# A graph network on one core: blocks of two heads in one double tile, moved by four DMAs, and keys loaded through SP's queue

## The chip, the core and the metric

The kernel runs on one NeuronCore of a Trainium2 chip. The core has TensorE (PE; its weight loads are listed as PEld), VectorE (DVE), ScalarE (ACT), GpSimd (POOL), SyncE (SP), which here only issues DMAs, and 16 DMA engines that all queues share. SP's DMAs are hardware-generated and appear as queue q1, POOL's are software-generated and appear as q0. The metric is the device time of one execution in microseconds; of several runs the median is taken.

## What is computed

Sixteen graphs of 1024 nodes with 256 features go through two layers. Layer 0 is masked attention with 8 heads of 32, layer 1 an edge softmax over the same adjacency, whose entries are 0 or 1 (so only the first of four edge kinds occurs). Cut to what matters:

```python
# layer 0
h = maximum(layernorm(x), 0)
Q, K, V = (h @ W.T + bias, split into 8 heads of 32)
scores = where(adj == 0, -inf, Q @ K.T * 32 ** -0.5)
x = x + (softmax(scores) @ V, heads joined) @ Wo.T + bo
# layer 1
h = maximum(layernorm(x), 0)
e = leaky_relu((h * a_0) @ h.T, 0.2)
x = x + softmax(where(adj == 1, e, -9e15)) @ h
```

## The kernel before

**Steps.** The work is cut into tiles of 128 rows, 8 a batch, 128 in all. After a prelude that projects the whole of batch 0, a loop of 129 steps runs (L838); step s has t = s % 8. In one step four things run beside each other, in an order written out by hand over h = 0 to 7 (L848 to L977): attention of tile s (`now`), the end of attention of tile s - 1 (`was`), layer 1 of the tile nine steps back (`edge`, and the one before it `edge_was`), and layernorm and projection of the tile nine ahead (`piece`, `piece_was`). A tail then does the last edge tiles alone (L984 to L1012). Each engine takes its instructions in the order in which they are written; nothing is reordered.

**One head.** `scores(h)` (L470) is two matmuls of 512 columns into one of two PSUM sides; heads 4 and 6 use side 1, which the edge tile shares, the others side 0. `softmax_max` (L482, DVE) masks and copies the scores to a tile `p`; `softmax_exp` (ACT) follows one h later. Two h later `p` has to be turned, so that PE can multiply it with V. There are two ways. Heads 2, 3, 6 and 7 go through PE and are copied out of PSUM by ACT (`turn_half`, L588). Heads 0, 1, 4 and 5 (`BY_BLOCKS`) are transposed in 32x32 blocks by DVE (`blocks_of`, L393) into a tile of the tag "blocks", and four DMAs on SP's queue (`placed`, L398) then put the blocks of each group of 32 partitions into their place in a tile "pT":

```python
for a in range(NB):
    nc.sync.dma_start(out=pT[:, a * NT * HD : (a + 1) * NT * HD], in_=blocks[a * HD : (a + 1) * HD])
```

Each of these DMAs moves 128 KB. Head 0 is turned at h = 2, head 1 at h = 3, head 4 at h = 6, head 5 at h = 7. `combine(0)` (L525; 64 matmuls, heads 0 to 3) stands at h = 7 of the same step, `combine(1)` (heads 4 to 7) at h = 3 of the next.

**The edge tile.** Its turned tile is made in the same way: `edge_was.turn_blocks` and `place_blocks` at h = 0, one more user of "blocks". A third user is `bend` (L663): at h = 3 ACT writes `less`, which has the tag "blocks" too, and POOL subtracts it in `leak` (L678). "blocks" has three buffers, taken in turn: edge, head 0, `less`, head 1, head 4, head 5. Behind `less` stands `keep(1)` (L643) on ACT, which copies a part of side 1 to `mirror`, and only then may `scores(4)` write side 1.

**POOL.** After `less` POOL runs `sel` (L678), the mask (L454), the split of the projected queries (`halve(1)`, L320), `prepare` (L612), the norms (`norm_of`, L146) and the split of the projected keys (`halve(0)`) of the next step; SP then writes those keys to DRAM (`kd`, L340) before it comes to the edge tile's placements.

**Keys.** Each batch has 8 key tiles of 512 KB, read back from DRAM by `load_key` (L372), on SP's queue for batch 0 and on POOL's for all others. `load_keys` (L841) spreads the eight over the last step of a batch (t = 7: keys 0 to 3, at h = 3 to 6) and the first of the next (t = 0: keys 4 to 7, at h = 0 to 4), by the list

```python
KEY_STEPS = (6, 9, 10, 13, 16, 20, 22, 24)
```

**Other DMAs of a step.** On SP: the query load (512 KB), two query writes (256 KB each), two key writes, the store of x1, the output. On POOL: adjacency (512 KB), two key writes, and three loads of x.

Of the kernel before, what the change touches and what calls it, by code (L numbers as in the profile page):

```python
# [8 lines left out]
F32 = mybir.dt.float32  # L9
# [8 lines left out]
P = 128  # L18
HEADS = 8
HD = 32  # L20
# [6 lines left out]
BY_BLOCKS = (0, 1, 4, 5)  # L27
# [7 lines left out]
FLOOR = 1e28  # L35


def by_chunk(place):
    return place.rearrange("p (c n) -> p c n", n=P)


@with_exitstack
def gnn_kernel(
# [18 lines left out]
    nc = tc.nc  # L62
    B, N, D = x.shape
    NT = N // P
# [124 lines left out]
        nc.vector.bn_aggr(out=mv, in_=st)  # L189


    qds, kds, vs, keysets, weights = {}, {}, {}, {}, {}

    class Piece:

# [4 lines left out]
        def __init__(self, b, first, n=1):  # L200
            self.b, self.first, self.n = b, first, n
            self.cols = slice(first * P, (first + n) * P)
            self.projected, self.halved, self.again, self.queries = [], [], [], []
            self.tags = ("xin", "h0", "hT", "halves", "hTm") if n == 1 else ("pT", "pT", "qt", "p", "blocks")

        def buffer(self, i, shape, dtype=F32):
            tag = self.tags[i]
            if tag == "pT":
                return ptp.tile(shape, dtype, tag=tag, name=tag)
            bufs = {"p": 4, "blocks": 3, "halves": 2 if self.n == 1 else 4, "qt": 2, "xin": 2}.get(tag, 1)  # L210
            return work.tile(shape, dtype, tag=tag, name=tag, bufs=bufs)

        def load(self, queue=nc.gpsimd):
# [158 lines left out]
    def load_key(b, h):  # L372
        kt = keys.tile([P, N], F32R, tag=f"k{h}", name=f"k{h}_{b}")
        c, r = divmod(h, GROUP)
        (nc.sync, nc.gpsimd)[b > 0].dma_start(
            out=kt.bitcast(F32),
            in_=kds[b][c, r * HD : (r + 1) * HD].rearrange("d w u n -> (d w u) n"),
        )
        keysets.setdefault(b, {})[h] = kt
# [10 lines left out]

        return rows.rearrange("(k b) n -> b k n", b=NB)

    def blocks_of(p):  # L393
        blocks = work.tile([P, NB, NT, HD], F32, tag="blocks", bufs=3)
        nc.vector.transpose(blocks.rearrange("p b j q -> p j b q"), p)  # L395
        return blocks.rearrange("p b j q -> p b (j q)")

    def placed(blocks, pT):  # L398
        for a in range(NB):
            nc.sync.dma_start(  # L400
                out=pT[:, a * NT * HD : (a + 1) * NT * HD], in_=blocks[a * HD : (a + 1) * HD]
            )
        return pT.rearrange("p (a j q) -> p j a q", a=NB, j=NT)


    h1s, x1ds, masks = {}, {}, {}
# [22 lines left out]
    class Attend:  # L429
# [65 lines left out]

        def turn(self, h, half):
            if half == 0:
                self.turned[h] = ptp.tile([P, NT, P], F32, tag="pT", name="pT")
            turn_half(self.probs[h][0], self.turned[h], half)

        def turn_blocks(self, h):
            self.blocks = blocks_of(self.probs[h][0])

        def place_blocks(self, h):
            self.turned[h] = placed(self.blocks, ptp.tile([P, N], F32, tag="pT", name="pT"))

        def reciprocals(self):

# [88 lines left out]
    class Edges:  # L597


        def __init__(self, b, t, last=False):  # L600
            self.b, self.t, self.last = b, t, last
            self.rows = slice(t * P, (t + 1) * P)
            self.side = sides[t % 2 if last else 1]
            self.tags = {"sel": ("p", 4), "pT1": ("pT", 7)} if last else {}
            if last and t % 2:
                self.tags |= {"ha": ("hT", 1), "x1b": ("x1", 1)}

# [55 lines left out]
        def bend(self):  # L663

            if not self.last:
                self.less = work.tile([P, N], F32, tag="blocks", name="less", bufs=3)
                nc.scalar.activation(self.less, self.sel, AF.Relu, scale=1 - 1 / SLOPE)  # L667

        def leak(self):
# [119 lines left out]
    with tc.manual_schedule():  # L789
# [195 lines left out]
        gone.turn_normed()  # L985
        gone.turned_normed()
        tiles = [edge_was, edge] + [edges_of(B * NT + LAG - NT + t) for t in range(1, NT)]
        for i in range(1, len(tiles) + 2):
            edge = tiles[i] if i < len(tiles) else None
            if edge:  # L990
                edge.score(0)
                edge.score(1)
            if i <= len(tiles):
                tiles[i - 1].turn_blocks()
                tiles[i - 1].place_blocks()
            if i >= 3:
# [12 lines left out]
            if i >= 2:  # L1009
                tiles[i - 2].gather(0)  # L1010
                tiles[i - 2].gather(1)
# [53 lines left out]
```

## Time and profile before

| | us |
|---|---|
| median of 3 runs (range) | 3232.47 (3231.46 to 3240.4) |
| the profiled execution | 3239.68 |
| its span, clock granted to TensorE | 3237.8, 0.979 |
| PE busy | 2972.1 (92%) |
| ACT, DVE, POOL busy | 2576.2, 2516.9, 2342.7 |
| first score matmul of the loop | at 66.5 |
| placements pT<-blocks on SP's queue | 2560 of 128 KB, median 3.5 from issue to landing |
| key loads on POOL's queue | 120 of 512 KB, median 7.1 |

A busy share is a mean over steps with different limits, so the profile is read here by steps: a step goes from the first score matmul (L474) of one tile to that of the next. Idle time before an instruction is listed with what ended it ("<-DMA pT<-blocks" is the landing of a placement). "SPq" is the issue of a DMA by SP; the time beside it is that of issuing, not of moving. In merged lines of a timeline, x12 is twelve issues in a row.

### The profile page before, as it was taken

The numbers are of one execution on the slowest core, as the hardware profiler recorded it, in microseconds if no ns is written. First come the engines' busy times: TensorE is split into PE (matmuls) and PEld (weight loads), VectorE is DVE, ScalarE is ACT, GpSimd is POOL, SyncE is SP. The second block draws the span as 40 slices with busy tenths as digits, with TensorE's granted clock in tenths as the row PEclk, the third lists the DMA queues.
The fourth block names the chain that finished last, engine by engine and source line by source line (L and its number), as shares of the span: only waits on it lengthen the run. The fifth ranks groups of instructions, "written<-read, shape, count | busy, mean of one in ns | idle before, by whom it ended". The sixth has DMA issues, their size and how long they took to land. (4 is left out here: it accounts for less than half of the span.)

```text
span 3237.8 us, 97791 instructions
## 1 busy us (share of the span) xinstructions
PE 2972.1 (92%) x36210; PEld 2211.2 (68%) x36210; DVE 2516.9 (78%) x4391; ACT 2576.2 (80%) x5157; POOL 2342.7 (72%) x4723
## 2 busy tenths in 40 slices
PE   5878989999899998999999898999989899898987
PEld 3766767667676776767767676776767677676663
DVE  3777868788787887878788787887878788787874
ACT  3887878888787887888888787887878788787871
POOL 2666777777777787777777777787777777776652
PEclk8999999999999999999999999999999999999999
DMA  6787777878878788788878878788888878878663
GB/s 227 222 257 216 232 243 235 256 229 240 248 226 278 223 240 257 232 272 235 260 230 239 258 231 272 220 240 252 234 262 235 262 221 250 258 225 259 186 171 93
DMA packets 747155, 762.91 MB, mean 236 GB/s; under 512 B 71280, under 2 KB 692208, under 8 KB 746672
## 3 DMA queue, kind: packets, MB, share of 16 engines
q1 hardware_dynamic: 678432, 542.34, 56.6%
q0 software_dynamic: 65040, 210.03, 20.6%
q8 instruction: 291, 4.77, 0.6%
q10 hardware_dynamic: 3200, 4.19, 0.4%
q14 instruction: 192, 1.57, 0.1%
HBM read 252.98 MB, written 167.77 MB: 130 GB/s over the span
## 5 line engine op out<-in xcount | busy, mean ns | idle before, releaser
L486 DVE CUSTOM_DVE_ANT_0 p<-s,neg 128x1024 f32<-128x1024 f32 x1024 | 1232.3, 1207 | 273.7 <-PE s L474 192.4
L494 ACT ACTIVATE p<-p,nmx 128x1024 f32<-128x1024 f32 x1024 | 1184.8, 1157 | 156.6 <-DVE nmx L486 154.6
L474 PE MATMUL s<-k,qt 128*128 128x512 f32 x2048 | 766.8, 456 | 145.0 <-DMA qt<-qd 53.5
L395 DVE STREAM_TRANSPOSE blocks<-p 128x1024 f32<-128x1024 f32 x520 | 644.8, 1240 | 152.7 <-DMA pT<-blocks 140.4
L594 ACT COPY pT<-trp 128x512 f32<-128x512 f32 x1024 | 548.4, 590 | 134.1 <-PE trp L593 133.7
L529 PE MATMUL acc<-pT,v 128*32 128x128 f32 x16384 | 552.7, 280 | 42.8 <-DMA pT<-blocks 41.1
L529 PEld LDWEIGHTS acc<-pT,v 128*32 128x32 f32 x16384 | 469.3, 112 | 157.8 <-issue 89.6
L593 PE MATMUL trp<-ident,p 128*128 128x128 f32 x4096 | 549.8, 278 | 2.3 <-ACT pT L594 2.1
L593 PEld LDWEIGHTS trp<-ident,p 128*128 128x128 f32 x4096 | 477.6, 142 | 93.1 <-ACT pT L594 28.8
L454 POOL TENSOR_SCALAR neg<-adj 128x1024 bf16<-128x1024 int32 x128 | 468.8, 3663 | 75.0 <-ACT neg L466 65.1
L700 PE MATMUL acc<-h,pT 128*32 128x256 f32 x8192 | 499.5, 383 | 10.7 <-DVE ot L709 7.8
L474 PEld LDWEIGHTS s<-k,qt 128*128 128x128 f32 x2048 | 326.5, 193 | 253.4 <-issue 87.6
L700 PEld LDWEIGHTS acc<-h,pT 128*32 128x32 f32 x8192 | 244.0, 110 | 216.4 <-issue 59.9
L678 POOL TENSOR_TENSOR sel<-sel,less 128x1024 f32<-128x1024 f32 x120 | 285.7, 2381 | 142.5 <-ACT less L667 142.5
L635 PE MATMUL s<-h1T,ha 128*128 128x512 f32 (+2 forms) x744 | 275.0, 493 | 2.6 <-ACT h1T L572 1.2
L523 ACT COPY recT<-acc 128x256 f32<-128x256 f32 x128 | 47.7, 373 | 205.3 <-PE acc L519 205.3
L494 ACT ACTIVATION_READ_ACCUMULATOR p<-p,nmx 128x1 f32 x1024 | 205.1, 200 | 0.0
L340 POOL DMA_DIRECT2D kd<-halves x240 | 172.1, 764 | 43.1 <-POOL halves L323 34.8
L323 POOL TENSOR_TENSOR halves<-full,halves 128x256 fp32r<-128x256 f32 x240 | 176.4, 735 | 20.6
L635 PEld LDWEIGHTS s<-h1T,ha 128*128 128x128 f32 x744 | 127.7, 192 | 72.0 <-issue 45.6
L273 PEld LDWEIGHTS acc<-hT,wkT 128*128 128x128 f32 x960 | 118.0, 194 | 66.7 <-ACT p L494 31.7
L676 POOL TENSOR_SCALAR less<-top 128x1 f32<-128x1 f32 x120 | 29.8, 248 | 176.7 <-DVE top L658 175.4
(132 smaller groups left out, 4526.9 us busy)
## 6 DMA issues: line engine op xcount, KB each, us to landing
pT<-blocks SPq DMA_DIRECT2D x2560, 128.0 KB, 3.5
qt<-qd SPq DMA_DIRECT2D x128, 512.0 KB, 4.7
adj<-in_adj POOLq DMA_DIRECT2D x127, 512.0 KB, 5.3
qd<-halves SPq DMA_DIRECT2D x240, 256.0 KB, 4.6
k<-kd POOLq DMA_DIRECT2D x120, 512.0 KB, 7.1
kd<-halves POOLq DMA_DIRECT2D x240, 128.0 KB, 3.5
kd<-halves SPq DMA_DIRECT2D x240, 128.0 KB, 3.8
xb<-in_x POOLq DMA_DIRECT2D x128, 128.0 KB, 3.5
```

Source lines behind the costliest of these rows:

```text
L323: nc.gpsimd.tensor_tensor(halves[:, :, 1], self.full, halves[:, :, 0].bitcast(F32), ALU.subtract)
L395: nc.vector.transpose(blocks.rearrange("p b j q -> p j b q"), p)
L454: nc.gpsimd.tensor_scalar(self.neg, self.adj, 0.0, MASKED, ALU.is_equal, ALU.mult)
L474: nc.tensor.matmul(self.ps[:, cols], lhsT=self.qt[:, h, :], rhs=keysets[self.b][h][:, cols], start=True, stop=True,)
L486: nc.vector.tensor_tensor_reduce(out=p, in0=sides[h in (4, 6)], in1=self.neg, scale=-SCALE, scalar=FLOOR, op0=ALU.add, op1=ALU.min, accum_ ...
L494: nc.scalar.activation(p, p, AF.Exp, bias=nmx, scale=-1.0, accum_out=self.sums[:, h : h + 1])
L529: nc.tensor.matmul(sums_place[r * HD : (r + 1) * HD, g * P : (g + 1) * P], lhsT=vs[self.b][:, j, place_of(h) : place_of(h) + HD], rhs=self ...
L593: nc.tensor.transpose(tr[:, j, :], p[:, jj * P : (jj + 1) * P], ident)
L594: copy(pT[:, half * 4 : half * 4 + 4, :], tr)
L635: nc.tensor.matmul(self.side[:, cols], lhsT=self.ha[:, c, :], rhs=h1T[:, c, cols], start=(c == 0), stop=(c == NC - 1),)
L678: nc.gpsimd.tensor_tensor(self.sel, self.sel, self.less, ALU.subtract)
L700: nc.tensor.matmul(sums_place[a * HD : (a + 1) * HD, :], lhsT=self.pT[:, j, a], rhs=h1s[self.b][:, j, :], start=(j == 0), stop=(j == NT - 1),)
```

## The change

- Heads 0 and 1, and 4 and 5, are turned into the two halves of one double tile ("pair", 8 KB a partition, one buffer). Nothing is moved after the first of the two; after the second, four DMAs of 256 KB move both, in rows of 2 KB instead of 1 KB, into a double tile "pairT" (two buffers).
- "pT" has 3 buffers instead of 7, "blocks" 1 instead of 3, for `less` and for the edge tile, which still moves its own blocks by four DMAs of 128 KB.
- All keys are loaded through SP's queue. `KEY_STEPS` is as before.
- The two first pieces of the prelude use halves of the double tiles; in the tail the edge tiles take turns in the halves of one "pair".

```diff
+    def pair(tag):
+        if tag == "pairT":
+            return ptp.tile([P, 2 * N], F32, tag=tag, name=tag, bufs=2)
+        return work.tile([P, 2 * N], F32, tag=tag, name=tag, bufs=1)
...
-            self.tags = ("xin", "h0", "hT", "halves", "hTm") if n == 1 else ("pT", "pT", "qt", "p", "blocks")
+            self.tags = ("xin", "h0", "hT", "halves", "hTm") if n == 1 else ("pairT", "pairT", "qt", "p", "pair")
...
-            if tag == "pT":
-                return ptp.tile(shape, dtype, tag=tag, name=tag)
-            bufs = {"p": 4, "blocks": 3, "halves": 2 if self.n == 1 else 4, "qt": 2, "xin": 2}.get(tag, 1)
+            if tag in ("pair", "pairT"):
+                if i not in shared:
+                    shared[i] = pair(tag)
+                half = by_chunk(shared[i], N)[:, self.first // self.n].bitcast(dtype)
+                return half.rearrange("p (a b) -> p a b", a=shape[1])
...
-        (nc.sync, nc.gpsimd)[b > 0].dma_start(
+        nc.sync.dma_start(
             out=kt.bitcast(F32),
...
-    def blocks_of(p):
-        blocks = work.tile([P, NB, NT, HD], F32, tag="blocks", bufs=3)
-        nc.vector.transpose(blocks.rearrange("p b j q -> p j b q"), p)
-        return blocks.rearrange("p b j q -> p b (j q)")
-
-    def placed(blocks, pT):
+    def blocks_of(p, blocks, i, n):
+        blocks = blocks.rearrange("p (b h j q) -> p h j b q", h=n, b=NB, j=NT)
+        nc.vector.transpose(blocks[:, i], p)
+
+    def placed(blocks, pT, n):
+        width = n * NT * HD
         for a in range(NB):
             nc.sync.dma_start(
-                out=pT[:, a * NT * HD : (a + 1) * NT * HD], in_=blocks[a * HD : (a + 1) * HD]
-            )
-        return pT.rearrange("p (a j q) -> p j a q", a=NB, j=NT)
+                out=pT[:, a * width : (a + 1) * width],
+                in_=blocks[a * HD : (a + 1) * HD].rearrange("s (b n) -> s b n", b=NB),
+            )
+        return pT.rearrange("p (a h j q) -> p h j a q", a=NB, h=n, j=NT)
...
-                self.turned[h] = ptp.tile([P, NT, P], F32, tag="pT", name="pT")
+                self.turned[h] = ptp.tile([P, NT, P], F32, tag="pT", name="pT", bufs=3)
...
         def turn_blocks(self, h):
-            self.blocks = blocks_of(self.probs[h][0])
+            i = BY_BLOCKS.index(h) % 2
+            if i == 0:
+                self.blocks = pair("pair")
+            blocks_of(self.probs[h][0], self.blocks, i, 2)
 
         def place_blocks(self, h):
-            self.turned[h] = placed(self.blocks, ptp.tile([P, N], F32, tag="pT", name="pT"))
+            if BY_BLOCKS.index(h) % 2:
+                pT = placed(self.blocks, pair("pairT"), 2)
+                self.turned[h - 1], self.turned[h] = pT[:, 0], pT[:, 1]
...
-            self.tags = {"sel": ("p", 4), "pT1": ("pT", 7)} if last else {}
+            self.tags = {"sel": ("p", 4), "pT1": ("pT", 3)} if last else {}
...
-                self.less = work.tile([P, N], F32, tag="blocks", name="less", bufs=3)
+                self.less = work.tile([P, N], F32, tag="blocks", name="less", bufs=1)
...
-        def turn_blocks(self):
-            self.blocks = blocks_of(self.sel)
+        def turn_blocks(self, place=None):
+            if place is None:
+                place = work.tile([P, N], F32, tag="blocks", name="blocks", bufs=1)
+            self.blocks = place
+            blocks_of(self.sel, place, 0, 1)
 
         def place_blocks(self):
-            self.pT = placed(self.blocks, self.buffer("pT1", [P, N]))
+            self.pT = placed(self.blocks, self.buffer("pT1", [P, N]), 1)[:, 0]
...
+        sets = by_chunk(pair("pair"), N)
...
-                tiles[i - 1].turn_blocks()
+                tiles[i - 1].turn_blocks(sets[:, i % 2])
```

More of the change, by code (lines that the diff above doesn't have):

```diff
@@ L35, with by_chunk @@
 FLOOR = 1e28
-def by_chunk(place):
-    return place.rearrange("p (c n) -> p c n", n=P)
+def by_chunk(place, n=P):
+    return place.rearrange("p (c n) -> p c n", n=n)
 @with_exitstack
@@ L189, in stats_of @@
         nc.vector.bn_aggr(out=mv, in_=st)
-    qds, kds, vs, keysets, weights = {}, {}, {}, {}, {}
+    qds, kds, vs, keysets, weights, shared = {}, {}, {}, {}, {}, {}
+    def pair(tag):
+        if tag == "pairT":
+            return ptp.tile([P, 2 * N], F32, tag=tag, name=tag, bufs=2)
+        return work.tile([P, 2 * N], F32, tag=tag, name=tag, bufs=1)
     class Piece:
@@ L203, in __init__ @@
             self.projected, self.halved, self.again, self.queries = [], [], [], []
-            self.tags = ("xin", "h0", "hT", "halves", "hTm") if n == 1 else ("pT", "pT", "qt", "p", "blocks")
+            self.tags = ("xin", "h0", "hT", "halves", "hTm") if n == 1 else ("pairT", "pairT", "qt", "p", "pair")
         def buffer(self, i, shape, dtype=F32):
             tag = self.tags[i]
-            if tag == "pT":
-                return ptp.tile(shape, dtype, tag=tag, name=tag)
-            bufs = {"p": 4, "blocks": 3, "halves": 2 if self.n == 1 else 4, "qt": 2, "xin": 2}.get(tag, 1)
+            if tag in ("pair", "pairT"):
[3 more added lines that the diff above has]
+                return half.rearrange("p (a b) -> p a b", a=shape[1])
+            bufs = {"p": 4, "halves": 2 if self.n == 1 else 4, "qt": 2, "xin": 2}.get(tag, 1)
             return work.tile(shape, dtype, tag=tag, name=tag, bufs=bufs)
```

## The prediction

> **What bounds the kernel now.** I read the table by stretches first, cut at the first score matmul (L474) of each of the eight steps of one batch, steps 72 to 79 of the loop. Columns: stretch, its length, then busy time of PE, PEld, DVE, ACT and POOL, the granted clock, the DMA share and GB/s.
>
> ```profile
> 1794.13:1824.87 30.74, 23.40 (x285) 18.28 (x286) 19.06 (x35) 19.65 (x40) 21.23 (x44) 0.89 0.85 291
> 1824.87:1849.19 24.32, 23.77 (x286) 16.91 (x283) 19.57 (x35) 20.64 (x44) 17.14 (x32) 1.00 0.77 230
> 1849.19:1872.77 23.58, 23.18 (x288) 17.11 (x284) 19.47 (x35) 20.47 (x43) 18.15 (x37) 1.00 0.80 240
> ...
> 1896.04:1919.03 22.99, 22.59 (x289) 17.05 (x285) 19.56 (x35) 20.03 (x41) 18.09 (x37) 1.00 0.79 232
> ...
> 1941.93:1964.41 22.48, 22.35 (x287) 16.77 (x284) 19.50 (x35) 20.02 (x41) 18.06 (x36) 1.00 0.77 221
> 1964.41:1987.77 23.36, 21.88 (x288) 16.96 (x284) 19.45 (x35) 20.11 (x41) 18.42 (x34) 1.00 0.90 267
> ```
>
> Two regimes are to be seen. In steps t = 1 to 6 PE is busy for all but about 0.4 us: TensorE sets the step. The first step of a batch (t = 0) has the same PE work and lasts 7 us longer. Who is late there, the waits say (engine and line, what it waited for, us in all, times, longest):
>
> ```profile
> DVE blocks L395 <- DMA pT<-blocks: 140.4, 80, 5.0
> PE s L474 <- DMA qt<-qd: 53.5, 22, 15.2
> PE acc L529 <- DMA pT<-blocks: 41.1, 25, 5.1
> PE s L474 <- DMA k<-kd: 39.9, 23, 3.9
> PE s L474 <- ACT mirror L649: 31.2, 83, 0.7
> ACT less L667 <- DMA pT<-blocks: 26.1, 9, 5.3
> ```
>
> PE waits for keys, placed blocks and queries; all come by DMA, and the DMA view of the stretch 1794 to 1825 us shows a share of 0.9 or more at 350 to 400 GB/s for its first 16 us, with 5.1 us instead of 3.6 from issue to landing of a placed block. I average the steps by their place, batches 1 to 14, from the same starts: t = 0 to 7 last 30.30, 24.46, 23.59, 23.27, 23.00, 23.14, 22.79 and 24.80 us, a batch 195.35.
>
> The third view is the timeline of step 76 (t = 4; start, us, engine, line), for a chain that does not bind today but will matter:
>
> ```profile
> 1898.87 0.74 POOL L323 TENSOR_TENSOR halves<-full,halves 128x256 fp32r<-128x256 f32 x1
> 1900.90 1.25 SPq L340 DMA_DIRECT2D kd<-halves  x2
> 1902.26 10.01 SPq L400 DMA_DIRECT2D pT<-blocks  x12
> ...
> 1905.65 1.05 ACT L667 ACTIVATE less<-sel 128x1024 f32<-128x1024 f32 x1
> 1906.60 0.57 ACT L649 COPY mirror<-s 128x512 f32<-128x512 f32 x1
> 1906.78 2.38 POOL L678 TENSOR_TENSOR sel<-sel,less 128x1024 f32<-128x1024 f32 x1 [1.23 <-ACT less L667]
> 1907.22 0.73 PE L474 MATMUL s<-k,qt 128*128 128x512 f32 x2 [0.40 <-ACT mirror L649]
> ...
> 1921.87 0.74 POOL L323 TENSOR_TENSOR halves<-full,halves 128x256 fp32r<-128x256 f32 x1
> ```
>
> The first four of the twelve placements from 1902.26 are the edge tile's. They land about 1907.8, after `less` has begun: `less` takes another of the three "blocks" buffers. PE's scores(4) waits for the mirror copy that stands behind `less` on ACT, and POOL's `sel` waits for `less`.
>
> **The change, part by part.**
>
> *Fewer placements.* Sixteen head placements a step become eight of 256 KB. Four cost SP 2.5 us in the timeline (0.64 each), so SP is free 5 us earlier a step; edge tiles keep four small ones. In step 76 SP came to the key writes (1900.90) 1.3 us after their data (1899.61); the time of heads 4's and 5's placements did that. This alone moves nothing in steps 1 to 6, since PE hides it. For the packets: the queues' rows give 56.6% of 16 engines' span for 542 MB on q1, 54 us of engine time per MB, and 51 on q0. At q0's price the 2 MB of heads would save 6 us of engine time a step, 0.4 us over 16 engines; I take 0 to 0.4, all under PE. [...]
>
> *DVE.* The 520 transposes of 1240 ns remain. Heads 1 and 5 wait for no buffer now; heads 0 and 4 wait until the single double tile has been read. Head 5 ends 0.6 us into the step, four issues follow to 3.2, and a 256 KB write lands 4.6 us after its issue (the row of qd), so 7.2; head 0 begins at 6.5 today. So 0.7 us, in place of 0.98 before head 1 in step 76. DVE is idle over 3 us a step: cost nothing, and 0.7 us a step if that cover were gone. PE's combine(1) at 8.6 still finds its data.
>
> *Keys on SP's queue.* 120 issues of 575 ns (69 us) and 25 us of waits leave POOL. What counts is when they go out: POOL issues keys 1 and 2 late, behind the mask (3.66 us) and the norms. On SP they stand behind the query load, some 4 to 5 us earlier, key 3 before the step ends. Keys 4 to 6 follow at the start of t = 0, with the key writes, the edge placements and the double placement queued behind them; key 0 waits for the last key writes, and then the pair's placement, 3 us away, stands behind it. In steps 7 and 0 a normal 5.3 MB each (the DMA view of step 76) and 4 MB of keys have to move: 14.7 MB, 38 us at 390 GB/s, beside 45.3 us of PE work (21.88 + 23.40). So the stall of t = 0 need not be, if the load is spread. [...]
>
> *"blocks" has one buffer, not three.* The order of the changed program's instructions shows `less` waiting for the four edge placements of its own step. This adds a wait with much behind it on ACT: the mirror copies (PE's scores(4)), the flag, exp(3); and POOL's `sel`. It closes a **loop**: from the end of `less` (1906.70) POOL works without a pause, sel, mask, halves, ha, norms, until the next halves end (1922.62): 15.92 us, the same in steps 2 to 6. Then SP's two key writes 1.36 and three placement spacings 1.92 (3.3 in all), landing 3.6, `less` 1.05. The sum is 23.9 us, whatever PE has to do. The landing is the uncertain term: 2.5 is the shortest block placement in the trace, 5.1 the median in the full queue of t = 0; I take 3.6, the median of step 76, since the same bytes go out in the same order.
>
> *pT from 7 to 3 plus two double ones; first pieces and tail in halves of double tiles.* A pT is freed by the combine before its next use (combine(0) ends the step, head 2 comes at h = 4). Cost 0; if one were short, a turn would wait for a combine, 2.2 us.
>
> *Sum.* t = 1: 24.2 (PE 23.8 and 0.4). t = 2 to 7: 23.9 each, 143.4. t = 0: the loop, one key issue ahead (0.6) and 5.1 instead of 3.6 to land: 26.0. A batch: 193.6 instead of 195.35, 1.75 us less, 14 times: 25. The last batch's edges have no key writes ahead; its first step gives 2 more at most, which I leave out. The profiled execution took 3239.7 us (span 3237.8, 1.9 around it), 7 over the median of the runs shown, 3232.5; the same saving against that gives **3207**.
>
> **Rivals.**
> - *The new wait wins (slower).* From a landing of 3.9 us the loop of 24.2 in all seven steps and 26 for the first eat the gain. At 4.3, a loop of 24.6: 172.2 + 26 = 198.2, 2.85 more a batch, 40 us: 3272. For it: 1 MB of pair goes out just ahead, and kd lands after up to 4 us there. Against: SP is 1.3 us earlier.
> - *The wait hardly binds.* With 3.1, a loop of 23.4: 24.2 + 23.55 + 5 x 23.4 + 25.5 = 190.25, 5.1 less a batch, 71 us: 3161. For it: queue and SP are emptier.
> - *The keys still collide.* One queue in order makes blocks wait behind keys; half of what t = 0 gives is lost, 28.2 instead of 26.0: 195.8, 0.45 more a batch: 3239. This is also the case that the change does not do what it says.
>
> **How the numbers follow.** Likeliest, 3195 to 3222: 0.36. Rival one 0.34; rival two 0.17; rival three 0.13. Faster is the first with rival two, less a little at its edge: 0.5; within 0.3% (10 us, about what a measurement of this kernel can tell) 0.14; slower 0.36. The range reaches over most of both sides: 3145 to 3290; the likeliest alone is 3195 to 3222.
>
> **What would show it.** Right: t = 0 shrinks to about 26 us; steps 2 to 7 all become equally long, near 23.9, with PE gaps behind the mirror copy and `less` waiting for the DMA of blocks in some hundred steps; DVE's wait for blocks falls under heads 1; POOL's L375 is gone. Wrong: steps 2 to 6 stay at 22.5 to 23.6 (no loop), or t = 0 stays near 30 (keys still late), or DVE waits long before head 0.

## The result, and the profile after

The changed kernel takes **3766.26 us** (median of four runs, 3761.83 to 3780.7) where the kernel before, run beside it, takes 3236.43 us: ratio **1.164, 95% interval 1.160 to 1.168**. The prediction was 3207 with a range to 3290, so it is wrong in sign and size. The profiled execution took 3768.68 us, its span is 3766.6 us, and the clock granted to TensorE fell from 0.979 to 0.926. The loop's place in the program is the same; only line numbers moved: scores are L483 now (L474 before), placements L408 (L400), turnings L403 (L395), `less` L681 (L667), the mirror copy L663 (L649), the key writes L348 (L340), the combine L543 (L529).

The stretches of the changed kernel, steps 72 to 79, cut as before (length, busy time of PE, PEld, DVE, ACT, POOL, granted clock, DMA share, GB/s):

```profile
2100.89:2130.76 29.87, 23.42 (x290) 17.04 (x286) 19.37 (x35) 19.77 (x40) 18.31 (x37) 0.94 0.93 305
2130.76:2158.75 27.99, 25.05 (x286) 18.20 (x283) 19.57 (x35) 21.07 (x44) 18.41 (x38) 0.94 0.71 193
2158.75:2188.56 29.81, 25.30 (x287) 19.00 (x283) 19.57 (x35) 20.90 (x43) 18.95 (x39) 0.89 0.70 183
...
2216.23:2243.00 26.77, 23.74 (x290) 18.07 (x286) 19.38 (x35) 20.14 (x41) 17.07 (x31) 0.94 0.72 185
...
2298.30:2327.97 29.67, 25.54 (x289) 20.02 (x285) 19.48 (x35) 20.15 (x41) 20.32 (x46) 0.83 0.88 248
```

The two regimes are gone. From t = 1 on no engine fills a step any more, the DMA share is lower than before (0.70 to 0.72 in the three rows shown of t = 1, 2 and 4, 0.77 to 0.80 before), and yet steps t = 1 to 6 of this batch are 3.7 to 6.2 us longer. By their place, batches 1 to 14, the steps t = 0 to 7 last 30.00, 28.55, 29.51, 27.69, 27.53, 29.06, 28.24 and 27.65 us, a batch 228.24 instead of 195.35. Batch 0, whose steps have no edge tile in the loop, grew too, from 20.5 to 25.9 us a step. The 32.89 us of 14 batches (460), 8 steps of batch 0 (43), batch 15 (17) and the tail (8) make up the whole 529 us between the two spans.

The waits of the changed kernel (engine, line, what it waited for, us in all, times, longest):

```profile
ACT less L681 <- DMA pT<-blocks: 398.0, 98, 7.9
DVE pair L403 <- DMA pairT<-pair: 352.5, 115, 6.3
...
PE s L483 <- ACT mirror L663: 284.3, 99, 4.9
...
PE acc L543 <- DMA pairT<-pair: 160.0, 95, 4.8
```

There are two kinds: `less` on ACT waits for the edge tile's placements (the wait that the prediction saw coming), and DVE (head 0) and PE (the combine) wait for the double placement (which it priced at nothing). The timeline of step 76 shows both; the step begins at 2216.23:

```profile
2215.61 1.24 DVE L403 STREAM_TRANSPOSE pair<-p 128x1024 f32<-128x1024 f32 x1
2216.91 3.98 SPq L408 DMA_DIRECT2D pairT<-pair  x4
2217.50 0.73 POOL L331 TENSOR_TENSOR halves<-full,halves 128x256 fp32r<-128x256 f32 x1
2220.99 3.18 SPq L348 DMA_DIRECT2D kd<-halves  x2
2224.28 2.97 SPq L408 DMA_DIRECT2D pT<-blocks  x4
2226.80 1.25 DVE L403 STREAM_TRANSPOSE pair<-p 128x1024 f32<-128x1024 f32 x1 [3.97 <-DMA pairT<-pair]
2226.81 0.30 PE L543 MATMUL acc<-pairT,v 128*32 128x128 f32 x2 [1.95 <-DMA pairT<-pair]
2229.61 1.06 ACT L681 ACTIVATE less<-sel 128x1024 f32<-128x1024 f32 x1 [3.67 <-DMA pT<-blocks]
2231.19 0.73 PE L483 MATMUL s<-k,qt 128*128 128x512 f32 x2 [1.08 <-ACT mirror L663]
```

SP issues the four placements of heads 4 and 5 from 2216.91 on; single ones show that the third and the fourth issue take 1.27 and 1.37 us instead of 0.6, and the last lands at 2226.68. That is 9.8 us after the first issue. At that moment DVE's head 0 and PE's combine(1) go on. SP reaches the key writes at 2220.99, 2.8 us after their data (2218.23), and needs 3.2 us for these two; so the edge tile's placements start at 2224.28 and `less` at 2229.61, 13.4 us into the step instead of 9.6 in the same step before.

### The profile page after: what moved, and what is told of

Read it like the earlier page. It is cut to its first block, busy times and chain, and to the rows that moved or that the text cites. A ratio compares the mean times of both kernels' runs of the same rounds, so it can differ in the third digit from the quotient of the medians.

```text
span 3766.6 us, 95108 instructions
## 1 busy us (share of the span) xinstructions
PE 3110.6 (83%) x36210; PEld 2331.7 (62%) x36210; DVE 2519.5 (67%) x4391; ACT 2597.2 (69%) x5157; POOL 2285.5 (61%) x4603
## 5 line engine op out<-in xcount | busy, mean ns | idle before, releaser
L483 PE MATMUL s<-k,qt 128*128 128x512 f32 x2048 | 815.9, 482 | 367.3 <-ACT mirror L663 284.3
L403 DVE STREAM_TRANSPOSE pair<-p 128x1024 f32<-128x1024 f32 x520 | 644.6, 1240 | 444.2 <-DMA pairT<-pair 352.5
L543 PE MATMUL acc<-pairT,v 128*32 128x128 f32 x8192 | 535.8, 287 | 205.2 <-DMA pairT<-pair 160.0
L543 PEld LDWEIGHTS acc<-pairT,v 128*32 128x32 f32 x8192 | 465.1, 115 | 306.8 <-issue 140.2
L483 PEld LDWEIGHTS s<-k,qt 128*128 128x128 f32 x2048 | 347.8, 205 | 489.2 <-ACT mirror L663 329.4
L607 PE MATMUL trp<-ident,p 128*128 128x128 f32 x4096 | 608.7, 298 | 26.3 <-ACT pT L608 26.2
L607 PEld LDWEIGHTS trp<-ident,p 128*128 128x128 f32 x4096 | 543.8, 155 | 122.1 <-ACT pT L608 39.1
L543 PE MATMUL acc<-pT,v 128*32 128x128 f32 x8192 | 535.8, 287 | 0.0
L681 ACT ACTIVATE less<-sel 128x1024 f32<-128x1024 f32 x120 | 126.8, 1057 | 474.6 <-DMA pT<-blocks 398.0
L543 PEld LDWEIGHTS acc<-pT,v 128*32 128x32 f32 x8192 | 454.0, 115 | 0.0
L649 PE MATMUL s<-h1T,ha 128*128 128x512 f32 (+2 forms) x744 | 272.8, 490 | 2.7 <-ACT h1T L586 2.4
L564 DVE TENSOR_TENSOR x<-acc,xb 128x256 f32<-128x256 f32 x128 | 54.4, 425 | 285.9 <-ACT full L326 215.6
L348 POOL DMA_DIRECT2D kd<-halves x240 | 172.2, 762 | 41.4 <-POOL halves L331 34.5
```

The lines of the kernel that those rows point to most:

```text
L348: queue.dma_start(out=kds[self.b][oc, :, :, twice, self.cols], in_=halves.rearrange("p (w n) -> p w n", w=2),)
L403: nc.vector.transpose(blocks[:, i], p)
L483: nc.tensor.matmul(self.ps[:, cols], lhsT=self.qt[:, h, :], rhs=keysets[self.b][h][:, cols], start=True, stop=True,)
L543: nc.tensor.matmul(sums_place[r * HD : (r + 1) * HD, g * P : (g + 1) * P], lhsT=vs[self.b][:, j, place_of(h) : place_of(h) + HD], rhs=self ...
L607: nc.tensor.transpose(tr[:, j, :], p[:, jj * P : (jj + 1) * P], ident)
L649: nc.tensor.matmul(self.side[:, cols], lhsT=self.ha[:, c, :], rhs=h1T[:, c, cols], start=(c == 0), stop=(c == NC - 1),)
```

## The experiments

**By themselves: how fast is such a move (runs 1 and 5)?** In run 1 nothing but SP's queue runs; in run 5 POOL's queue loads 512 KB at a time beside some of the bursts.

> The placements by themselves: nothing is computed (the output is zeros), SP's queue alone moves 4 MB in each of six forms, once as one long burst and three times as a burst of 1 MB. Forms: rows of 1 KB as in the kernel before (32 partitions read, 128 KB each); the same out of a double tile; rows of 2 KB as in the changed kernel (32 partitions read, 256 KB each); these with the groups in the order 0, 2, 1, 3; 256 KB with 1 KB rows; 256 KB with 2 KB rows read from all 128 partitions. Theory one (a transfer that reads 32 partitions is slow in itself once 256 KB go out every 0.64 us): the third form lands its fourth placement about 10 us after the first issue, as in step 76 of the changed kernel (9.8), with packets near 147 ns, while the one that reads 128 partitions lands it by about 5 to 6 us with packets near 84 ns; the first form lands 1 MB at SP's spacing, 8 x 0.64 + 3, about 8 us. Rival (the transfer is slowed by the other traffic of the step, not by its own form): the third form alone has packets of 84 ns and lands by 5 to 6 us, like the sixth. [...]

The fourth placement of 256 KB out of 32 neighbouring partitions lands 7.1 to 7.3 us after the first issue, its packets last 84 ns (median), 148 on average and over 300 the slowest tenth, and SP's third and fourth issue take 1.2 and 1.6 us. Read from 128 partitions, the same bytes in the same rows land 4.3 us after the first issue, nearly every packet takes 84 to 93 ns, every issue 0.5 to 0.6 us. In a long burst one of 256 KB comes down every 1.14 us from neighbours (15 in 17.14 us, **229 GB/s**) and every 0.68 us (SP issues one every 0.65) from 128 partitions. In the order 0, 2, 1, 3 it is every 1.05 us, 9% more; its three short bursts took 6.4, 6.7 and 7.6 us. 128 KB placements, at SP's 0.65 us, ask for 201 GB/s, stay under this and land after 2.6 us each. Eight of them are down after 7.1 us, no later than four of 256 KB. So theory one holds in this: the move out of 32 neighbouring partitions is slow by itself, though not the 10 us of the kernel. Rows of 1 KB in a DMA of 256 KB are as slow (1 MB after 7.2 to 7.4 us), so the row's length is not what made the difference here.

> Placements by themselves again, nothing computed (the output is zeros). 256 KB out of 32 partitions in rows of 2 KB to 128 partitions, once from 32 neighbouring partitions (as in the changed kernel), once from every fourth partition (32 partitions spread over all 128); and 128 KB in rows of 1 KB. Then each form behind one load of 512 KB and two writes of 256 KB on the same queue and one load of 512 KB on POOL's. Theory one (neighbouring partitions share the way out of SBUF): spread over all, the transfer keeps SP's spacing, issues take 0.6 us, the fourth lands 5 us after the first issue (7.2 from neighbours), packets 84 ns. Rival (32 source partitions, or four rows out of each, are slow wherever they lie): the same 7.2 in both. Behind the other traffic the fourth placement of 256 KB lands 2 to 3 us later than alone, that is about as late as in the kernel (9.8).

```python
in_=src[a * HD : (a + 1) * HD]    # neighbours
in_=src[a::NB]                    # every fourth partition
```

These are the DMA views of two long bursts of 4 MB with SP's queue alone, neighbours first (run 1), then every fourth partition (run 5), each in 40 slices (of the 21.1 and 13.6 us); the last line of each gives the median from issue to landing:

```profile
GB/s 0 0 74 105 136 245 120 93 303 307 210 260 245 210 206 210 225 284 256 163 148 256 326 214 210 322 264 214 136 237 342 233 148 202 249 280 206 182 136 0
dst<-src SPq DMA_DIRECT2D x16, 256.0 KB, 4.7
```

```profile
GB/s 0 0 0 145 386 374 386 368 386 380 392 380 386 386 386 386 386 386 373 380 386 362 392 380 380 392 374 361 398 374 392 380 386 380 386 343 18 0 0 0
dst<-src SPq DMA_DIRECT2D x16, 256.0 KB, 2.7
```

Each DMA of both reads 32 partitions, 8 KB of each, and writes the same rows. Spread over all 128 they run at 380 GB/s from start to end, and the fourth of a short burst lands 4.4 us after the first issue (5.1 in one burst, where the second issue came late), against 7.1 to 7.3 out of neighbours. So it was where the 32 partitions lie that counted here, not how many they are. Out of neighbours the rate starts at some 100 GB/s and then swings between 90 and 340.

The other traffic was not tested as it was meant. All nine of POOL's loads went out early, beside the neighbours' bursts at the start of the run, and SP's load had landed before the placements began. Beside one of POOL's loads the fourth placement out of neighbours lands 7.6 to 8.3 us after the first issue; right behind two writes of 256 KB alone, 7.4 to 7.6. What makes it 9.8 us in step 76 (9.2 is the median of heads 4 and 5 over batches 1 to 14, 8.2 in batch 0) is open by 1 to 2 us.

**The keys alone (run 2).** The kernel before with only `load_key` changed.

```diff
-        (nc.sync, nc.gpsimd)[b > 0].dma_start(out=kt ...
+        nc.sync.dma_start(out=kt ...
```

> The kernel before with one part of the change: the keys on SP's queue. Theory one (keys are not what slowed the changed kernel): within 40 us of the kernel before; if the prediction's step on keys holds, t = 0 falls from 30.3 to about 26 us and the time by 14 x 4, to about 3180. Rival (keys on SP's queue hold up the placements behind them): t = 0 and t = 7 grow by 5 us or more each, 3236 + 14 x 10, about 3380.

Ratio 1.010 (1.006 to 1.014). Step t = 7 falls from 24.80 to 22.74, t = 0 grows from 30.30 to 34.32, where PE waits 7.3 us for keys (2.6 before). SP issues key 3 only 5.1 us into the step and key 7 at 22.1, each behind the placements that are written ahead of it. So the keys cost 28 us, within the 40 of theory one and a sixteenth of the loss; t = 0 did not fall to 26 us.

**The wait of `less` alone (run 3).** The kernel before; `less` and the edge tile's blocks share one buffer, heads keep two.

```diff
-  self.less = work.tile([P, N], F32, tag="blocks", name="less", bufs=3)
+  self.less = work.tile([P, N], F32, tag="blocks1", name="less", bufs=1)
-  self.blocks = blocks_of(self.sel)             # tag "blocks", bufs=3
+  self.blocks = blocks_of(self.sel, "blocks1", 1)
```

> The kernel before with one part of the change: less and the edge tile's blocks share one buffer (heads keep two, the sum is three as before), so less has to wait for the edge placements of its own step. Theory one (this wait is late only because the double placements hold up SP and the queue): the loop of the prediction, 23.9 us a step, 3 us a batch more than now, 3236 + 14 x 3, about 3280. Rival (this wait is the main cause): steps of 27 us and more, 3236 + 113 x 3.5, above 3600.

Ratio **1.114** (1.109 to 1.119): the rival is right, this wait is dear without any double placement. A batch takes 219.20 us; batch 0, which has no edge tile, is unchanged (20.9 a step). `less` waits 345.7 us in 99 steps and starts at 11.1 to 12.1 us in t = 1 to 6. SP's timeline of step 44, which starts at 1207.75, shows why:

```profile
1207.44 1.36 SPq L400 DMA_DIRECT2D pT<-blocks  x2
1208.84 0.60 SPq L555 DMA_DIRECT2D x1d<-x  x1
1209.55 2.49 SPq L400 DMA_DIRECT2D pT<-blocks  x4
1212.14 1.24 SPq L340 DMA_DIRECT2D kd<-halves  x2
1213.49 8.75 SPq L400 DMA_DIRECT2D pT<-blocks  x11
```

The four from 1209.55 are head 5's. Only after them, 4.4 us into the step, SP comes to the key writes and then to the edge tile. In steps t = 2 to 6 this start lies 4.6 to 5.1 us into the step in the kernel before, in this one and in the changed one (medians), and here 1.3 to 3.2 us after the key data: it follows heads 4 and 5, not POOL. The prediction had it at once behind POOL.

**Head 5 behind the edge tile (run 9).** As run 3, with head 5's placements issued after the key writes and the edge placements of the next step.

```diff
-                    turning.place_blocks(th)
+                    if th != 5:
+                        turning.place_blocks(th)
...
                         edge_was.place_blocks()
+                    if was:
+                        was.place_blocks(5)
```

> The third run again (the kernel before, less and the edge tile's blocks in one buffer), with one thing moved: SP issues the four placements of head 5 after the key writes and the edge tile's placements of the next step, not before them. Theory (the loop that set that run's steps goes from scores(4) over the step's end, head 5's turning and its four issues on SP to the key writes, which start 4.8 us into the step in every kernel): the key writes start right after their data, the loop is POOL's, 15.92 + 0.2 + 1.36 + 1.94 + 3.5 + 0.1 + 1.06 = 24.1 us, about 3270 to 3340. Rival (this wait is dear wherever head 5's placements stand): 3560 to 3650, as in the third run.

Ratio 1.126 (1.124 to 1.129). The expected time is missed by far, yet the wait did move as the theory says. The waits of this run:

```profile
PE acc L529 <- DMA pT<-blocks: 425.8, 122, 8.4
...
ACT less L667 <- DMA pT<-blocks: 88.9, 20, 8.2
```

The key writes start 0.03 to 1.2 us behind their data and `less` stands where it stood before the change (9.0 to 10.9 us into the step), but head 5 now lands 13.7 us into step 44, and combine(1), which precedes scores(4) on PE, waits for it. One of the two has to be late on SP; this run could not tell the price of the buffer.

**Without head 5's placements (runs 13 and 14).** So they were left out, in two kernels, one with the shared buffer and one without.

```diff
-                    turning.place_blocks(th)
+                    if th == 5:
+                        turning.turned[5] = turning.turned[4]
+                    else:
+                        turning.place_blocks(th)
```

> The third run (the kernel before, less and the edge tile's blocks in one buffer) without the placements of head 5: the combine takes head 4's turned tile for head 5 as well, so the output is another, DVE, ACT and PE have the same instructions, SP has four issues and the queues 512 KB less a step. Theory (less is late there because SP comes to the key writes and the edge placements only after head 5's four issues): the key writes start within 0.3 us of their data and the steps are POOL's loop, 15.92 + 0.3 + 1.36 + 1.94 + 3.4 + 0.1 + 1.06 = 24.1 us, 60 to 110 us above the same kernel with three shared buffers, about 3280 to 3330. Rival (the single buffer is dear whatever stands ahead on SP): 250 us or more above it.

> The kernel before without the placements of head 5 (the combine takes head 4's turned tile), to measure the thirteenth run against: buffers as before. PE sets most steps: 3195 to 3240 by every theory.

Ratios 1.049 (1.047 to 1.052) with one buffer and 0.984 (0.982 to 0.987) with three, the latter 9 us below its expected range; 209 us between the medians (3395.3 and 3185.9), between what the two theories gave. With one buffer SP starts the key writes 0.03 us behind their data (median), and t = 2 to 6 last 24.0 to 25.1 us. The sum of the loop with what this run shows (landing 3.9) is 15.92 + 0.03 + 1.32 + 1.92 + 3.9 + 0.1 + 1.06 = 24.25. So POOL's loop is real and about as long as the prediction said; it takes 1.7 us a step from t = 2 to 6 (24.7 against 23.05) and 5.5 us more in t = 0 and 7 together. The other 150 us of run 3 go with head 5's four placements. This run takes away their issues on SP and their 512 KB at once; that SP then starts right behind the data speaks for the issues, but the two were not tested apart.

**The same bytes in eight DMAs (run 4).** The changed kernel; each half of the double tile goes by itself.

```diff
-        for a in range(NB):
-            nc.sync.dma_start(
-                out=pT[:, a * width : (a + 1) * width],
-                in_=blocks[a * HD : (a + 1) * HD].rearrange("s (b n) -> s b n", b=NB),
-            )
+        for i in range(n):
+            for a in range(NB):
+                nc.sync.dma_start(
+                    out=pT.rearrange("p (a h x) -> p h a x", a=NB, h=n)[:, i, a],
+                    in_=blocks[a * HD : (a + 1) * HD].rearrange("s (b h x) -> s h b x", b=NB, h=n)[:, i],
+                )
```

> The changed kernel with the double tile moved by eight DMAs of 128 KB in rows of 1 KB instead of four of 256 KB in rows of 2 KB; tiles, buffers, the moment of the first issue and the bytes stay. Theory one (the 2 KB form is slow in itself: 147 ns a packet, where two of 1 KB take 2 x 54): the placements land some 1.5 us earlier and SP's key writes and the edge placements are no longer slowed, less comes about 1 us earlier, about 3600 to 3680. Rival (what counts is that both heads' bytes start only after the second head, whatever their form): 5.1 us of issues instead of 3.9 ahead of the key writes, 3766 to 3880.

Ratio **1.065** (1.060 to 1.070), 318 us under the changed kernel and better than expected. The expectation was wrong in one thing that decides how this is read: the first issue does move. The first four DMAs read the first head's half only, so SP waits for that head's turning and issues them 1.47 us before the step instead of 0.68 us into it. The run undoes two things, the size and the late start. The placements of heads 4 and 5 are then down 7.2 us into the step, at 9.85 in the changed kernel (medians of batches 1 to 14). Batch 0 is back at 20.5 us a step. Stretches of two steps of batch 0, the changed kernel first, then this one:

```profile
142.88:168.02 25.14, 18.90 (x214) 15.51 (x210) 16.01 (x29) 16.98 (x36) 13.85 (x30) 0.91 0.68 183
168.02:194.47 26.45, 19.77 (x213) 16.10 (x210) 17.15 (x30) 18.22 (x38) 13.85 (x30) 0.82 0.66 176
```

```profile
126.84:147.42 20.58, 18.13 (x214) 14.79 (x210) 16.59 (x29) 17.64 (x37) 13.58 (x31) 0.92 0.76 229
147.42:168.01 20.59, 18.15 (x214) 14.80 (x211) 16.61 (x30) 17.63 (x37) 14.01 (x31) 0.92 0.76 221
```

PE is busy 0.8 and 1.6 us longer in the changed kernel, at a clock of 0.91 and 0.82 instead of 0.92; the rest of the 4.6 and 5.9 us are gaps, and the DMA rate is lower, not higher.

**`less` with a buffer of its own**, in both forms (runs 6 and 7); 4 KB of it are paid for with two "pT" instead of three.

```diff
-  ... tag="pT", name="pT", bufs=3)
+  ... tag="pT", name="pT", bufs=2)
-  ... tag="blocks", name="less", bufs=1)
+  ... tag="blocks", name="less", bufs=2)
...
-  place = work.tile([P, N], F32, tag="blocks", name="blocks", bufs=1)
+  place = work.tile([P, N], F32, tag="blocks", name="blocks", bufs=2)
```

> The changed kernel with eight DMAs of 128 KB for the double tile (as in the fourth run) and two buffers for blocks, so that less waits for no placement of its own step; paid for with two pT instead of three. What is left of the change: both heads start after the second, one pair, keys on SP. Theory (the form of the transfers and the wait of less are all, the keys cost 30 us, the bunching nothing): the time of keys alone, 3260 to 3300. Rival (bunching, or the single pair, costs as well): above 3350.

> The changed kernel, four DMAs of 256 KB as in the change, but two buffers for blocks (less waits for no placement of its own step) and two pT instead of three. Theory (the 256 KB form hurts by itself too, as batch 0 shows, where no less waits: 25.9 us a step instead of 20.5): 3550 to 3650. Rival (the form hurts only by making the placements that less waits for late): 3260 to 3330.

With eight DMAs: ratio **0.995** (0.993 to 0.998), a little faster than the kernel before, and below what was expected. With four of 256 KB: 1.117 (1.115 to 1.120), as expected. Again the eight start early, so the first of the two says nothing on what bunching would cost. Together with run 4 and the changed kernel this is a table of two by two, as ratios to the kernel before:

| | `less` waits for the edge tile | own buffer |
|---|---|---|
| four of 256 KB, after the second head | 1.164 | 1.117 |
| eight of 128 KB, four of them early | 1.065 | 0.995 |

The form (size and late start together) costs 12.2% alone, the wait 7.0% alone, both together 17.0%, less than their sum. Without them nothing of the loss is left. How the form works alone, the waits of run 7 say:

```profile
DVE pair L403 <- DMA pairT<-pair: 370.9, 148, 6.4
ACT less L681 <- DVE top L672: 323.9, 107, 6.5
...
PE acc L543 <- DMA pairT<-pair: 172.8, 95, 4.9
```

`less` waits for no placement there, but for DVE's maximum of the edge tile (`top`), which stands behind head 0, and head 0 waits for the pair: so `less` still starts 12.3 us into the step (median of t = 1 to 6; 13.7 in the changed kernel, 9.8 before).

**Another order (run 8).** The changed kernel with `for a in (0, 2, 1, 3)`.

> The changed kernel, only the order of the four placements is 0, 2, 1, 3 instead of 0, 1, 2, 3 (double tile and edge tile). By themselves four of 256 KB landed 6.6 us instead of 7.2 after the first issue in this order. Theory (two neighbouring transfers out of the same half of the partitions share the same way): 0.6 us less twice a step on the chain, 3766 - 113 x 0.6 to 1.2, that is 3630 to 3700. Rival (the way out is not what makes them late in the kernel): 3750 to 3780.

Ratio 1.142 (1.139 to 1.144), 64 us under the changed kernel and, at 3702 us, just above the expected 3630 to 3700. The placements of heads 4 and 5 are down at 9.24 instead of 9.85 us. So 0.61 us of landing is worth 64 us, 0.57 us in each of 113 steps; the 2.62 us between the changed kernel and the run with eight DMAs are worth 318, 2.8 us a step. Both would fit a step that follows this landing about one to one. But `less` starts earlier in both as well, 13.1 and 11.4 us into the step instead of 13.7, so these runs do not tell the two waits apart.

**Keys again, and a version that beats both (runs 10 to 12 and 15 to 18).** In the run with eight DMAs and `less` of its own, SP is free at the end of a step: head 4's placements stand one h later in its order than in the kernel before, and keys 1 to 3 go out 6.5, 5.8 and 1.3 us before step t = 0 begins. In the run with the keys alone, keys 1 and 2 go out 4.9 and 4.1 us before it and key 3 5.1 us into it. In all the runs below that have eight DMAs, four of the eight start early, as in run 4, so none of them tests the bunching.

> The kernel before with keys 0 to 3 (those of t = 7) on SP's queue and keys 4 to 7 (those of t = 0) on POOL's. Theory (keys on SP help t = 7, where they don't stand behind POOL's mask, by 2 us a batch, and hurt t = 0, where they stand behind placements, by 4): 3236 - 14 x 2, about 3205 to 3225. Rival (the 4 us of t = 0 come from the same bytes being moved, not from where the keys of t = 0 stand): 3250 to 3280.

> The sixth run (eight DMAs of 128 KB, two buffers for blocks, keys on SP) with keys 4 to 7 on POOL's queue. If keys behind placements are what holds t = 0, below the sixth run by 1 to 3 us a batch, 3185 to 3215; if the bunching had already cured that (t = 0 is 28.9 us there, 34.3 with the keys alone), the same as the sixth run, 3220 to 3240, or a little more.

> The sixth run with all keys of later batches on POOL's queue, as in the kernel before. What is left of the change is then only that both heads of a pair are moved after the second. Theory (bunching itself costs nothing and gains nothing): 3230 to 3250, the kernel before. If the sixth run's gain comes from keys on SP that meet fewer placements on their way: the gain is lost, 3236 or more; if it comes from the bunching: below 3226.

> The sixth run once more, with more rounds and beside the next: 3220 to 3235, 0.3 to 0.6% under the kernel before.

> The sixth run with the keys of t = 0 issued earlier on SP's queue (KEY_STEPS 16, 18, 20, 22 instead of 16, 20, 22, 24). PE waits 2.5 us a batch for keys in t = 0 there. If what makes them late is where they stand on SP, 1 to 2 us less a batch: 14 to 28 us under the sixth run, about 3200 to 3212. If the queue is simply full in t = 0: the same time, 3220 to 3235.

> The sixteenth run with the keys of t = 0 still earlier on SP's queue (KEY_STEPS 15, 16, 18, 20). If they are late for their place on SP alone, another 0.5 to 1 us a batch, 3180 to 3192; if the transfers of t = 7 and t = 0 then meet and delay placements, 3200 to 3230.

> The kernel before with the key times of the sixteenth run (KEY_STEPS 16, 18, 20, 22), keys on POOL's queue as before. If early keys gain by themselves, 14 to 28 us here too, 3210 to 3225; if they gain only where SP's queue has room for them (both heads moved after the second, keys on SP), 3230 to 3250.

| | ratio (interval) | t = 7 | t = 0 |
|---|---|---|---|
| before, keys 0 to 3 on SP | 1.000 (0.998 to 1.002) | 22.51 | 31.95 |
| eight DMAs, own `less`, keys 0 to 3 on SP | 1.001 (1.000 to 1.003) | 22.78 | 30.25 |
| the same, keys on POOL | 1.002 (1.000 to 1.003) | 23.34 | 30.41 |
| the same, keys on SP (run 6 again) | 0.997 (0.995 to 0.999) | 22.96 | 29.49 |
| the same, keys on SP, steps 16, 18, 20, 22 | **0.988** (0.985 to 0.990) | 23.03 | 27.29 |
| the same, steps 15, 16, 18, 20 | 0.986 (0.983 to 0.990) | 22.92 | 26.96 |
| before, keys on POOL, steps 16, 18, 20, 22 | 0.999 (0.997 to 1.002) | 25.31 | 30.28 |

Keys on SP pay only in the version in which SP is free for them, and earlier keys only there: 40 us under the kernel before (3196.4 and 3236.6); in the kernel before they were tried on POOL's queue alone. Of the keys that run 16 moves, two go out nearly as in run 15 (11.6 and 12.9 us into t = 0 on average, 11.8 and 13.0 there) and the last 7 us earlier (13.4 instead of 20.6); PE's wait for keys in t = 0 falls from 3.0 to 1.2 us. Half of the keys on SP gains nothing in either place, so both expectations of run 10 missed, and in run 11 the one of a gain. The next step earlier is worth nothing more that could be measured (run 17, 3199 us, just under the upper of its two expected ranges). Three steps of the version with steps 16, 18, 20, 22, t = 0, 1 and 3 of one batch:

```profile
1772.17:1799.12 26.95, 22.18 (x289) 16.71 (x285) 19.38 (x35) 19.77 (x40) 18.57 (x39) 1.00 1.00 333
1799.12:1823.45 24.33, 23.78 (x286) 16.92 (x282) 19.57 (x35) 20.65 (x44) 17.89 (x35) 1.00 0.75 217
1847.80:1871.07 23.27, 22.87 (x289) 17.21 (x285) 19.59 (x35) 20.28 (x42) 18.12 (x37) 1.00 0.81 239
```

PE fills t = 1 and 3 again, and t = 0 is near the 26.0 of the prediction.

## Why the prediction was wrong, step by step

- *What bounds the kernel now*: right, and what was left after both faults were removed is bound by it again.
- *Fewer placements*: wrong. SP did not become free 5 us earlier. Four issues fewer save 2.5 us a pair in number, but the third and fourth of 256 KB take 1.3 us each, and SP came to the key writes as late as before (4.8 us into the step). The packets' gain of 0 to 0.4 us is a loss: one of 2 KB takes 147 ns on average in the changed kernel (median 84), two of 1 KB on that queue took 108 before. Larger rows by themselves brought nothing either: in run 1 DMAs of 256 KB were down after 7.1 to 7.3 us in rows of 2 KB and after 7.2 to 7.4 in rows of 1 KB.
- *DVE and the combine*: **this is the first step that failed**, "four issues follow to 3.2, and a 256 KB write lands 4.6 us after its issue (the row of qd), so 7.2", and with it "cost nothing" and "PE's combine(1) at 8.6 still finds its data". The row of qd reads 128 partitions, a placement reads 32 neighbours; same size, another transfer. Issues went on to 4.7 and the last landed at 9.85 us. Head 0 then waits 3.2 us instead of 0.7, and combine(1) 1.35 us, where 0 stood. In the versions with eight DMAs the landing is 7.1 to 7.2 and head 0's wait 0.5 to 0.7: from the landing on the sum was right, though those versions come to this landing by an earlier start. Two things made it late, that no byte moves before the second head is turned (2.15 us later than in run 4) and that the move takes over 7 us even alone. Spread over all partitions it took 4.4 alone; by that, as an estimate, it would land 5.1 us into the step and the late start would be harmless. That no run changed the start alone with four of 256 KB, or the spread within the kernel, or gave "pair" a second buffer, so that head 0 need not wait, is a gap: this split is argued from the times, not shown.
- *"blocks" has one buffer*: **the second step that failed**. The loop was found, and POOL's 15.92 us between `less` and the next key data hold (15.9 to 16.0 for t = 1 to 6 in the changed kernel and in runs 3, 4, 6, 7 and 13). What failed is the 0 between that data and the key writes, "SP is free 5 us earlier": SP was held by heads 4 and 5, 1.2 to 3.2 us in run 3 and 2.3 to 3.7 in the changed kernel (medians of t = 1 to 6). Then 1.36 for the key writes became about 3 in the changed kernel, behind the slow placements. Term by term, from the end of one `less` to the next (steps t = 2 to 6 of batches 1 to 14, means): POOL 15.95, SP late 2.73, key writes 3.08, spacing of the placements 2.07, landing 3.45, 0.13 before `less`, `less` 1.06, together 28.5 us, where the prediction had 15.92, 0, 1.36, 1.92, 3.6, 0 and 1.05. So two terms make the difference, and the landing, which it called the uncertain one, held, although the line read for it was not read quite right: the last of step 76 landed at 1908.30 and not about 1907.8, 4.0 us after its issue. And PE's clock, which no term held, fell from 0.979 to 0.926 over the run (below).
- *Keys on SP's queue*: wrong by itself (34.3 us for t = 0 instead of 26.0), since the keys stand behind placements there; nearer (28.9 and 29.5 in runs 6 and 15, 27.3 with earlier keys) once SP's order lets them pass. Keys on SP made t = 0 4.0 us longer in the kernel before (run 2) and 0.9 us shorter with eight DMAs and `less` of its own (run 15 against run 12), and with all keys on SP it lasts 34.3 us in one program order and 28.9 in another: what counted here was the place in SP's order.
- *pT*: right; even two instead of three are no loss that shows in run 6.
- *Sum*: 193.6 us a batch was forecast; 193.24 is what run 6 has (193.66 again in run 15), in which neither the form nor the wait is left. That is luck: run 6 does not have the loop, so its steps t = 2 to 7 last 22.9 to 23.8 us where 23.9 was forecast, and its t = 0 lasts 28.9 where 26.0 was. Of the single terms, POOL's 15.92, the landing and t = 1 (24.35 for 24.2) stood; both faults lie in transfers that were priced by the wrong row or the wrong start.
- *Rivals*: the first named the right wait for one of the two faults, and the right sign, but its reason (a later landing, 4.3 us for 3272) is not what happened: the landing stayed at 3.5 us (median of t = 1 to 6) and the start was late. The second (the wait hardly binds) is refuted by run 3. The third (keys collide) is what run 2 shows by itself, 28 us, but in the changed kernel t = 0 is no longer than before. That DVE's head 0 and the combine might wait for the pair was only a sign to look for, not a rival.

## What to carry to other kernels

Price a transfer by a row that reads and writes the same partitions, not one of the same size; alone, in long bursts, moves out of 32 neighbouring partitions ran at 200 to 250 GB/s here (201 in 128 KB, as fast as SP issued them, 229 in 256 KB, 250 in the order 0, 2, 1, 3), and those spread over all at 380. When several small DMAs are merged, ask what was overlapped by their being apart: the first head's bytes used to travel while the second was turned. When a new wait closes a loop, walk the loop over every in-order queue in it (here SP's), and take the moment at which the queue gets to the instruction from the timeline, not the moment at which its data is ready.

## What the runs showed of the hardware that was not expected

**Where a transfer reads.** Four DMAs of 256 KB, each out of 32 partitions, were down after 7.1 to 7.3 us from neighbours and after 4.4 (5.1 in one burst) from every fourth partition; in long bursts they ran at 229 GB/s (run 1) and at 380, SP's spacing (run 5). The order 0, 2, 1, 3 gave 9% in the long burst alone and 64 us in the kernel. Out of neighbours the long burst of run 1 started at about 100 GB/s for its first 1.5 us.

**SP's issue slows down with the transfers.** An issue of 0.6 us took 1.2 to 1.6 us when transfers of 256 KB from neighbours were two or three deep (the third and fourth of a burst, run 1), up to 2.1 beside POOL's loads (run 5) and 1.3 to 1.4 in step 76, and what stood behind it on SP was late by as much.

**TensorE's clock.** In run 3 PE's time from scores(4) to the next step is 11.82 us after short gaps and 13.39 after many longer ones, with the same matmuls. Two stretches just after such gaps, of 2.07 and 2.39 us (the column ahead of the last two is the granted clock):

```profile
1172.50:1174.50 2.00, 2.00 (x15) 1.44 (x13) 0.30 (x3) 2.00 (x7) 1.92 (x2) 1.00 0.78 195
1222.60:1224.60 2.00, 2.00 (x9) 1.72 (x7) 0.41 (x2) 1.49 (x4) 1.92 (x2) 0.50 0.82 202
```

Of the gaps before scores(4) in t = 1 to 6 of that run, 1 of 25 below 2.12 us was followed by the slow clock, 25 of 41 between 2.12 and 3.15, and all 18 above. So where the slow clock (0.50 in the second row) followed, a wait of 2 to 3 us on PE cost 1.6 us more than itself (13.39 against 11.82); in the changed kernel the slow clock followed 64 of the 77 gaps above 2.12 us in the same place (but not three of 3.4 to 3.9 us).
